# A planned recurrence with attention work in its gaps: a bar on long GpSimd operations, new guesses for DMA, deeper buffers at the start

## The chip, the cores and the metric

The kernel runs on one core of one Trainium2 chip. The metric is the device time of one launch in microseconds (us); lower is better. The engines are TensorE (PE, with its weight loads shown apart as PEld), VectorE (DVE), ScalarE (ACT), GpSimd (POOL) and SyncE (SP, which here issues every DMA). Each engine works through its own list of instructions in the order in which they were written and waits at the head of that list for what it needs.

## The reference, cut to what matters

Eight images of 56x56 positions and 256 channels pass through three layers; `_gn` and `_ln_t` are normalizations over groups and over channels.

```python
x = x + _L0_conv_ref(_gn(x), ...)                  # attention over 4 chosen regions of 8x8
t = _to_tokens(x)                                  # (8, 3136, 256)
t = t + _L1_attn_ref(_ln_t(t), ...)                # each token looks at 7 neighbours
t = t + _L1_ffn_ref(_ln_t(t), ...)                 # a recurrence over the 3136 tokens
# the recurrence, for all 8 images at once
i_t = sigmoid(xi_t + h @ V_i)
g_t = tanh(xg_t + h @ V_c)
o_t = sigmoid(xo_t + h @ V_o)
c_new = h * c + i_t * g_t                          # f_t isn't used
h_new = o_t * tanh(c_new)
```

In the first layer each of 49 regions takes the 4 regions whose mean keys fit best. Each of the 64 queries of a region, in each of 8 heads, keeps the 32 largest of 256 scores, and a softmax over those weighs the values. A depthwise 3x3 convolution of the values is added before the output projection.

## The kernel before, in words

**Units.** The image is cut into 7 rows of 7 regions (448 tokens each). A unit is one such row of one image, and the units run through all 8 images before the next row: 56 units. For a unit the kernel loads the row (`xn`), projects queries and values, writes the values to DRAM and reads them back three times shifted (`lines`, then `vshift`), convolves them with 24 matmuls on PE (`convolve`), and handles 7 regions (`region`: gather keys and values by DMA, scores on PE, eight rounds of MAX8 and MATCH_REPLACE8 per pair of heads on DVE, three Exp on ACT, a subtraction `pe<-pe,left` of 128x256 on POOL, transposes and products on PE). Behind it come the output projection, the attention over 7 neighbours and the input part of the gates, `gates`, which adds a bias on POOL (`gs<-gs,bu`) and writes the result to DRAM (`xgd`). I call all of this row work.

**The start.** For each image `norm_and_route` first reads the image in 7 chunks of 448 KB for statistics (`stats`), then in 7 chunks again (`keys_values`): a chunk `xchunk` is normalized on DVE, four matmuls make its keys (`ks`) and eight its values, ACT copies these out as four tiles `vs` and SP writes each to DRAM (`vd<-vs`). `xchunk`, `ks` and `vs` have two buffers each. The norm of the images is spread over the first units.

**The recurrence.** One step has a chain of six operations: 16 matmul records that add `h @ V` to a PSUM bank (`r_sum`), a DVE transpose (`r_tr`), a tanh on ACT (`r_cell<-r_tr`), a DVE scan (`r_c`), a tanh on ACT (`r_tc`), and a DVE operation that makes the new h (`r_hs`). Beside the chain, POOL makes the next step's product h*c (`r_cell<-r_hs,r_half`), which the next scan reads; I call it POOL's part. The terms `xgd` are loaded eight tokens at a time (`r_gin`) by SP and copied into the PSUM bank by ACT (`place_terms`). From step 2688 on, when only the recurrence is left, the matmuls for o are done apart (`step_apart`). `follow` records the steps of a row when the row's terms have been recorded, so a step at a multiple of 448 needs what the last unit of a row has written.

**The planner.** Nothing is written to the engines directly. `_Plan.record` collects every operation with its reads and writes, a guess `held` of how long it occupies its engine and a guess `late` of when its result is there (`_time`). `_Plan.run` then walks through a model time and hands each free engine the first ready operation by rank: the recurrence has rank 0, its six operations are marked `chain`, row work has rank 1. An operation that isn't of the chain is taken only if its end lies before the time at which the chain is expected to need that engine, plus `SLACK`. For POOL the expected time is that of the next chain operation on DVE with more than one tile read, which are the scan and the `r_hs` operation. Where PE would idle for over 250 ns a small matmul into `spare` is written. `at` counts the chain operations handed out, so `at % 6` is the place within a step: 0 behind `r_hs`, 1 behind the matmuls, 4 behind the scan. What comes out is one fixed order for each engine; on the chip the guesses no longer count, only the order and the real waits.

All recorded operations carry line 290 in the profile, so groups are told apart by their tiles.

Of the kernel before, what the change touches and what calls it, by code (L numbers as in the profile page):

```python
# [10 lines left out]
F32 = mybir.dt.float32  # L11
# [46 lines left out]
HOP = 70  # L58
FAR = 10**12
FILL = 250  # L60
SLACK = {"PE": 120, "DVE": 120, "ACT": 60, "POOL": 60, "SP": 1000}


def _shape_of(shape, pattern, sizes):
# [37 lines left out]
def _time(engine, name, view, reads, args, kw):  # L102

    n = max([_count(v) for v in [view] + reads])
    if engine == "SP":
        return 650, 2600 + n // 2
    if engine == "PE":
        held = 160 if name == "transpose" else 5 * _count(view) // 3 + 110
        return held, held + 200
    if engine == "POOL":  # L110
        t = 180 + 15 * n // 7
        return (1050, 1050) if ALU.pow in args else (t + 90, t)
    if engine == "ACT":
        t = 5 * n // 7 + 100
        if kw.get("accum_out") is not None:
            return t + 150, t + 260
        if isinstance(kw.get("bias"), _View) or view.buf.banks:
            return t + 120, t + 200
        return t + 20, t + 110
    held = 25 * n // 24 + 60  # L120
    if name == "reciprocal":
        return 20 * n // 3 + 60, 20 * n // 3 + 150
    if name == "transpose":
        return held + 40, held + 120
    if name == "tensor_tensor_scan":
        return 2 * n + 80, 2 * n + 170
    if name == "match_replace":
        return held + 65, held + 150
    if name == "scalar_tensor_tensor":
        return held + 20, held + 100  # L130
    return held, held + 90
# [97 lines left out]
class _Plan:  # L229
# [112 lines left out]
    def run(self, tc, fill):  # L342
        ops = self.ops
        for tag in self.tags.values():
            for i, buf in enumerate(tag):
                kin = [b for b in tag[:i] if b.stream == buf.stream][-1:] if buf.free else tag[i - 1 : i]
                before = [(b.users[0], 0) for b in kin]
                if i >= buf.bufs and not buf.free:
                    before += [(u, None) for u in tag[i - buf.bufs].users]
                for u, gap in before:  # L350
                    for v in buf.users:
                        if u is not v:
                            g = gap
                            if g is None:
                                g = u.held if u.engine == v.engine else u.late + HOP
                            u.before[v] = max(g, u.before.get(v, 0))
        for op in ops:
            op.open, op.due = 0, 0
        for op in ops:
            for b in op.before:  # L360
                b.open += 1
        engines = ("PE", "DVE", "ACT", "POOL", "SP")
        free = dict.fromkeys(engines, 0)
        later = {e: [] for e in engines}
        ready = {e: [] for e in engines}
        chain = [o for o in ops if o.chain]
        at, made, events = 0, {}, []

        def opened(op):
            heappush(later[op.engine], (op.due, op.rank, op))  # L370
            heappush(events, op.due)

        for op in ops:
            if not op.open:
                opened(op)
        done, now = [], 0

        def expected(engine):


            t = None
            for k in range(at, min(at + 7, len(chain))):
                op = chain[k]
                if t is None:
                    if op.open:
                        break
                    t = max(op.due, now)
                else:
                    p = chain[k - 1]
                    t += p.late + (HOP if p.engine != op.engine else 30)  # L390
                if op.engine == engine or engine == "POOL" and op.pair:
                    return t
            return FAR

        filled = 0
        while len(done) < len(ops) + filled:
            moved = False
            for e in engines:
                if free[e] > now:
                    continue  # L400
                while later[e] and later[e][0][0] <= now:
                    _, rank, op = heappop(later[e])
                    insort(ready[e], (rank, op))
                if not ready[e]:
                    continue
                until = expected(e) + SLACK[e]
                for i, (rank, op) in enumerate(ready[e]):
                    if not op.chain and now + op.held > until:
                        continue
                    if any(b.free and not self._room(b, made, now) for b in op.takes):  # L410
                        continue
                    del ready[e][i]
                    op.start = now
                    free[e] = now + op.held
                    heappush(events, free[e])
                    heappush(events, now + op.late + HOP)
                    done.append(op)
                    for b in op.takes:
                        if b.free:
                            made.setdefault(id(b.tag), []).append(b)  # L420
                    for b, gap in op.before.items():
                        b.due = max(b.due, now + gap)
                        b.open -= 1
                        if not b.open:
                            opened(b)
                    if op.chain:
                        at += 1
                    moved = True
                    break
            if not moved and free["PE"] <= now:  # L430

                due = min([expected("PE")] + [op[0] for op in later["PE"][:1]])
                if FILL < due - now < FAR // 2:
                    op = _Op()
                    op.trace, op.start = [fill], now
                    filled += 1
                    done.append(op)
                    free["PE"] = now + FILL
                    heappush(events, free["PE"])
                    moved = True  # L440
            if not moved:
                while events and events[0] <= now:
                    heappop(events)
                if not events:
                    raise RuntimeError("the plan has stopped")
                now = heappop(events)
        self.length = now
        with tc.manual_schedule():
            for op in done:
                for t in op.trace:  # L450
                    t()
# [25 lines left out]
def _layers(ctx: ExitStack, tc, a, out):  # L477
# [154 lines left out]
    def norm_and_route(b, im):  # L632
# [1 line left out]


        def chunk(p):
            xc = two.tile([P, 2, ROW], F32, name="xchunk")
            nc.sync.dma_start(
                xc, xt[b, :, p * ROW : (p + 1) * ROW].rearrange("(k q) s -> q k s", k=2)
            )  # L640
            return xc
# [67 lines left out]
        def keys_values(p):  # L709
            xn = chunk(p)  # L710
            normalize(im, xn)
            ks = two.tile([P, NWIN, 2, S], F32, name="ks")
            for m in range(2):
                pk = bank()
                for k in range(2):
                    nc.tensor.matmul(
                        pk[:, :ROW], w0[:, k, C + m * P : C + (m + 1) * P],
                        xn[:, k, :], start=(k == 0), stop=(k == 1),
                    )
                nc.scalar.activation(  # L720
                    ks[:, :, m, :], pk[:, :ROW].rearrange("p (q s) -> p q s", s=S),
                    AF.Identity, bias=b0[:, 2 + m : 3 + m],
                )
            nc.sync.dma_start(
                im["kd"][p * NWIN : (p + 1) * NWIN].rearrange("q p s -> p q s"),
                ks.rearrange("p q k s -> p q (k s)"),
            )
            for i in range(NQB):
                pv = bank()
                for k in range(2):  # L730
                    nc.tensor.matmul(
                        pv[:QB, :C], xn[:, k, i * QB : (i + 1) * QB], w0[:, k, 2 * C :],
                        start=(k == 0), stop=(k == 1),
                    )
                vs = two.tile([QB, C], F32, name="vs")
                nc.scalar.copy(vs, pv[:QB, :C])
                t0 = p * ROW + i * QB
                nc.sync.dma_start(im["vd"][t0 : t0 + QB], vs)
# [773 lines left out]
```

## Time and profile before

| what | value |
|---|---|
| median of 3 runs | 9912.33 us (9910.28 to 9922.73) |
| profiled execution | 9902.77 us, its span 9901.1 us |
| 0 to 1500 us (before the recurrence) | PE busy 1239.49 us, DVE 1052.58 us, granted clock 0.90 |
| 1500 to 8890 us (row work and recurrence) | PE busy 6891.83 us, DVE 6562.68 us, POOL 2691.74 us |
| 8890 us to the end (recurrence alone) | PE busy 872.89 us, DVE 432.97 us |
| steps of the recurrence | 3136 |

The busy times come from the profile's table by stretches of the span. Busy PE includes the `spare` matmuls, which do nothing for the result. A mean duration of a group can hide two populations, so places where it matters are looked at in the timeline, whose columns are start in us, length in us, engine, line, operation, output<-inputs, shape and count, and in brackets how long the engine had been idle and who ended that.

### The profile page before, as it was taken

Reading aid. Unit: us, or ns where it says so; the run is one execution under the profiler, and the core shown is the slowest. Engines: PE = TensorE matmul, PEld = TensorE weight load, DVE = VectorE, ACT = ScalarE, POOL = GpSimd, SP = SyncE. Lnnn points to the kernel's source line nnn. Section 1 sums busy time; section 2 is a strip of 40 time slices with the busy share of each in tenths; the row PEclk is TensorE's granted clock in tenths of the full one; section 3 lists DMA queues with packets and bytes.
Section 4 is the critical chain, followed back from the end, with each engine's and each line's share of the span. In section 5 each row is a group of like instructions: output and inputs, shape, how many; then the busy total and the mean of one; then the engine's idle time right before and its main releaser. Section 6 shows DMA issues by size and latency. Waiting matters only on the chain.

```text
span 9901.1 us, 320002 instructions
## 1 busy us (share of the span) xinstructions
PE 9004.2 (91%) x111782; PEld 5270.8 (53%) x111782; DVE 8048.2 (81%) x32969; ACT 5863.0 (59%) x22855; POOL 3193.8 (32%) x7550
## 2 busy tenths in 40 slices
PE   6888889999999999999999999999999999998888
PEld 4445445555555555555545555555555545557777
DVE  5686688999998999989989899898988888874444
ACT  3444456666666666666666666666666666654444
POOL 1222233333333333333333333333333333331111
PEclk9989889999999999999999999999999999999999
DMA  5544423233233232332323323233232222220000
GB/s 156 150 131 132 121 82 86 75 80 82 76 82 81 71 83 77 81 81 71 84 74 81 81 72 86 74 81 79 74 85 76 72 73 79 75 53 21 21 21 19
DMA packets 838243, 786.81 MB, mean 79 GB/s; under 512 B 94734, under 2 KB 794244, under 8 KB 836628
## 3 DMA queue, kind: packets, MB, share of 16 engines
q1 hardware_dynamic: 836628, 766.33, 29.1%
q8 instruction: 884, 14.48, 0.6%
q14 instruction: 731, 5.99, 0.2%
HBM read 527.08 MB, written 238.88 MB: 77 GB/s over the span
## 4 chain that ended last, share of the span: by engine, by line
DVE 46%; PE 16%; ACT 12%; DMA 5%; issue 5%; SPq 1%; POOL 1%; DVEq 0%; ACTq 0%; POOLq 0%
DVE left L290 13%; DVE top L290 10%; PE r_sum L290 9%; DVE r_c L290 7%; DVE r_tr L290 7%; ACT r_cell L290 5%; PE mm L290 5%; DVE r_hs L290 4%; DMA vshift<-lines 2%; ACT r_tc L290 2%; DMA lines<-v 2%; PE pt_av L290 1%; DVE st L290 1%; PE spare L604 1%; ACT et L290 1%
## 5 line engine op out<-in xcount | busy, mean ns | idle before, releaser
L290 PE MATMUL r_sum<-r_v,r_hs 128*8 128x192 f32 (+1 forms) x57376 | 2650.4, 307 | 496.1 <-DVE r_hs L290 439.1
L290 POOL TENSOR_TENSOR r_cell<-r_hs,r_half 128x16 f32<-128x16 f32 x3136 | 722.6, 230 | 4643.2 <-DVE r_hs L290 2588.8
L604 PE MATMUL spare<-ident 128*32 128x128 f32 x15904 | 2208.1, 277 | 1.5 <-POOL ident masks.py:199 1.5
L290 ACT ACTIVATE r_cell<-r_tr 128x48 f32<-128x48 f32 (+2 forms) x3587 | 911.7, 259 | 2156.4 <-DVE r_tr L290 2069.5
L290 PEld LDWEIGHTS r_sum<-r_v,r_hs 128*8 128x8 f32 x57376 | 1233.5, 89 | 1739.1 <-DVE r_hs L290 1397.5
L290 DVE MATCH_REPLACE8 left<-top,left 128x256 f32<-128x256 f32 x4704 | 1899.5, 407 | 0.2 <-issue 0.2
L604 PEld LDWEIGHTS spare<-ident 128*32 128x32 f32 x15904 | 1596.3, 110 | 471.9 <-issue 373.2
L290 DVE MAX8 top<-left 128x8 f32<-128x256 f32 x4704 | 1841.1, 406 | 1.4
L290 DVE STREAM_TRANSPOSE r_tr<-r_sum 128x192 f32<-128x192 f32 (+2 forms) x3587 | 1231.9, 350 | 631.1 <-PE r_sum L290 607.0
L290 DVE TENSOR_TENSOR_SCAN r_c<-r_cell 128x48 f32<-128x48 f32 x3136 | 945.5, 302 | 542.3 <-ACT r_cell L290 382.3
L290 POOL TENSOR_TENSOR pe<-pe,left 128x256 f32<-128x256 f32 x1568 | 1142.1, 733 | 731.2 <-ACT left L290 590.7
L290 ACT ACTIVATE r_tc<-r_c 128x16 f32<-128x16 f32 x3136 | 701.1, 224 | 508.9 <-DVE r_c L290 469.9
L290 ACT COPY r_sum<-r_gin 128x384 f32<-128x384 f32 (+2 forms) x1795 | 807.7, 450 | 14.1 <-DMA r_gin<-xgd 7.8
L290 ACT ACTIVATE pe<-sc,nmax 128x256 f32<-128x256 f32 x1568 | 684.9, 472 | 173.0 <-DVE left L290 103.4
L290 PE MATMUL pt_av<-ident,pe 128*128 128x128 f32 x3136 | 690.5, 297 | 91.2 <-POOL pe L290 67.2
L290 ACT ACTIVATE left<-left,nmax 128x256 f32<-128x256 f32 x1568 | 749.1, 500 | 35.5 <-DVE left L290 26.3
L290 DVE SCALAR_TENSOR_TENSOR r_hs<-r_cell,r_tc 128x16 f32<-128x16 f32 x3136 | 587.9, 187 | 188.8 <-ACT r_tc L290 183.7
L290 PE MATMUL mm<-wu,xlT 128*112 128x512 f32 (+2 forms) x1856 | 728.1, 509 | 3.2 <-ACT gs L290 2.5
L290 ACT ACTIVATE et<-top,nmax 128x32 f32<-128x32 f32 x1568 | 497.3, 318 | 332.8 <-DVE top L290 325.4
L290 DVE MAX8 top<-sc 128x8 f32<-128x256 f32 x1568 | 618.2, 412 | 78.6 <-PE sc L290 75.2
L290 ACT COPY pts<-pt_av 128x256 f32<-128x256 f32 x1568 | 566.0, 361 | 169.5 <-PE pt_av L290 166.8
L290 ACT ACTIVATE r_half<-r_c 128x16 f32<-128x16 f32 x3136 | 651.4, 208 | 0.0
(128 smaller groups left out, 11793.0 us busy)
## 6 DMA issues: line engine op xcount, KB each, us to landing
kg<-kd SPq DMA_DIRECT2D x1568, 64.0 KB
vg<-vd SPq DMA_DIRECT2D x1568, 64.0 KB
vshift<-lines SPq DMA_DIRECT2D x336, 232.0 KB
xgd<-gs SPq DMA_DIRECT2D x224, 336.0 KB
r_gin<-xgd SPq DMA_DIRECT2D x1568, 48.0 KB
xchunk<-xt SPq DMA_DIRECT2D x112, 448.0 KB
lines<-v SPq DMA_DIRECT2D x112, 290.0 KB
xn<-xh SPq DMA_DIRECT2D x56, 560.0 KB
```

What stands on the lines that cost most here:

```text
L290: method(*[v.real() if isinstance(v, _View) else v for v in args], **{k: v.real() if isinstance(v, _View) else v for k, v in kw.items()},)
L604: raw.tensor.matmul(spare[:32, :P], ident[:, :32], ident, start=True, stop=True, skip_group_check=True)
```

## The change

Four edits, all in the planner and in three buffer counts:

- In `_Plan.run`, an operation of POOL with a guessed length over 400 ns isn't taken while `at % 6 > 3` (behind the scan, before the `r_hs` operation), nor while a counter `tied` is below `at // 6`. `tied` counts POOL's operations of rank 0 outside the chain.
- `SLACK` of PE goes from 120 to 60 ns.
- The guess for a DMA of n elements per partition goes from 2600 + n/2 to 2400 + 9n/4 ns.
- `xchunk` has 4 buffers, `ks` 3 and `vs` 4, in place of 2 each.

```diff
-SLACK = {"PE": 120, "DVE": 120, "ACT": 60, "POOL": 60, "SP": 1000}
+LONG = 400
+SLACK = {"PE": 60, "DVE": 120, "ACT": 60, "POOL": 60, "SP": 1000}
...
     if engine == "SP":
-        return 650, 2600 + n // 2
+        return 650, 2400 + 9 * n // 4
...
-        filled = 0
+        filled = tied = 0
...
                     if not op.chain and now + op.held > until:
                         continue
+                    if e == "POOL" and op.held > LONG and (at % 6 > 3 or tied < at // 6):
+
+                        continue
...
                     if op.chain:
                         at += 1
+                    elif e == "POOL" and op.rank[0] == 0:
+                        tied += 1
...
-            xc = two.tile([P, 2, ROW], F32, name="xchunk")
+            xc = two.tile([P, 2, ROW], F32, name="xchunk", bufs=4)
...
-            ks = two.tile([P, NWIN, 2, S], F32, name="ks")
+            ks = two.tile([P, NWIN, 2, S], F32, name="ks", bufs=3)
...
-                vs = two.tile([QB, C], F32, name="vs")
+                vs = two.tile([QB, C], F32, name="vs", bufs=4)
```

No operation of the computation is added or removed. Of the engines' lists, all but PE's hold the same operations in another order; PE's has 255 `spare` matmuls fewer (7697 for 7952).

## The prediction

> **What bounds the kernel now.** I read the busy times by stretch first, then the waits of the middle stretch, then the timeline where the longest waits stand.
>
> ```profile
> 0.00:1500.00 1500.00, 1239.49 (x8038) 711.87 (x8042) 1052.58 (x3975) 677.82 (x2039) 395.97 (x724) 0.90 0.46 129
> 1500.00:8890.00 7390.00, 6891.83 (x84875) 3817.68 (x84864) 6562.68 (x27133) 4752.23 (x18559) 2691.74 (x6368) 1.00 0.30 77
> 8890.00:9900.00 1010.00, 872.89 (x18896) 741.20 (x18884) 432.97 (x1862) 432.98 (x2259) 106.06 (x458) 1.00 0.09 21
> ```
>
> Behind stretch and length stand busy PE, PEld, DVE, ACT, POOL, the granted clock, the DMA share and GB/s. Before 1500 us PE is the busiest; from then on the recurrence never stops, so its 3136 steps are the path. I took the start and length of all six chain operations of every step from the trace. With the medians of the stretch (r_hs to matmuls 55 ns, matmuls 837, 67 to the transpose as the shortest usual gap, 366, 94, tanh 268, 101, scan 258, 34, tanh 223, 32, r_hs 174) a step takes 2509 ns; the mean is 2752. Over steps 50 to 2685 the excess is some 630 us: 169 in front of the matmuls, 21 in them, 146 in front of the transpose, 135 inside the scan, 41 inside r_hs, the rest in small parts. The last 451 steps take 1005 us and the change touches nothing there.
>
> The 169 us are three things. Six waits of 10 to 12 us (63 us in all) stand where a new row's first terms are needed, every 448 steps:
>
> ```profile
> 2707.08 0.35 SPq L290 DMA_DIRECT2D xgd<-gs  x1
> ...
> 2708.58 0.16 DVE L290 SCALAR_TENSOR_TENSOR r_hs<-r_cell,r_tc 128x16 f32<-128x16 f32 x1
> ...
> 2713.37 2.68 SPq L290 DMA_DIRECT2D r_gin<-xgd  x8
> ...
> 2718.64 0.90 ACT L290 COPY r_sum<-r_gin 128x384 f32<-128x384 f32 x2 [2.08 <-DMA xgd<-gs]
> ...
> 2719.18 0.84 PE L290 MATMUL r_sum<-r_v,r_hs 128*8 128x192 f32 x16 [1.80 <-ACT r_sum L290]
> ```
>
> From the write of the terms to their use pass 12.1 us, and the write stands one step ahead of the use. Next, 51 waits over 0.5 us make 70 us; most look like this:
>
> ```profile
> 3208.36 0.44 DVE L290 SCALAR_TENSOR_TENSOR r_hs<-r_cell,r_tc 128x16 f32<-128x16 f32 x1
> ...
> 3210.61 1.16 PE L290 MATMUL mm<-vshift,diag 96*32 96x448 f32 x8 [3.44 <-DMA vshift<-lines]
> ...
> 3212.62 1.30 PE L290 MATMUL r_sum<-r_v,r_hs 128*8 128x192 f32 x12
> ...
> 3214.32 0.38 DVE L290 STREAM_TRANSPOSE r_tr<-r_sum 128x192 f32<-128x192 f32 x1 [4.13 <-PE r_sum L290]
> ```
>
> The convolution stands in PE's list before its data has landed, the step's matmuls are queued behind it, and then run at half speed (1.9 us for 0.84): that is the 21 us. The waits name it:
>
> ```profile
> DVE r_tr L290 <- PE r_sum L290: 264.9, 345, 6.3
> ...
> PE mm L290 <- DMA vshift<-lines: 78.2, 50, 4.1
> ```
>
> What is left of the 169, waits of 5 to 500 ns, is 36 us. At the start each chunk of keys and values has this cycle:
>
> ```profile
> 79.50 0.65 ACT L290 COPY vs<-mm 112x256 f32<-112x256 f32 x2 [2.16 <-DMA vd<-vs]
> ...
> 79.92 3.27 PE L290 MATMUL mm<-xchunk,w 128*128 128x448 f32 x8 [1.31 <-ACT vs L290]
> ...
> 83.03 3.73 PE L290 MATMUL mm<-w,xchunk 128*112 128x256 f32 x16
> ...
> 88.06 3.27 PE L290 MATMUL mm<-xchunk,w 128*128 128x448 f32 x8 [1.29 <-ACT vs L290]
> ```
>
> 8.14 us per chunk for 7.0 us of PE. The slow scans are those that meet a long POOL operation:
>
> ```profile
> 5003.66 0.73 POOL L290 TENSOR_TENSOR pe<-pe,left 128x256 f32<-128x256 f32 x1 [1.24 <-ACT left L290]
> ...
> 5003.85 0.64 DVE L290 TENSOR_TENSOR_SCAN r_c<-r_cell 128x48 f32<-128x48 f32 x1 [0.15 <-ACT r_cell L290]
> ...
> 5005.11 0.23 POOL L290 TENSOR_TENSOR r_cell<-r_hs,r_half 128x16 f32<-128x16 f32 x1 [0.72 <-DVE r_hs L290]
> ```
>
> The scan is held until 0.10 us behind POOL's end. The long operation stands in POOL's list ahead of the r_cell of the same step, and its inputs are there early, so nothing holds it back until that step's r_hs.
>
> **The bar on long POOL operations.** Matched to the planner's list, 529 of the 535 slow scans (over 290 ns) and all 191 slow r_hs (over 200 ns) meet a long operation that was handed out at place 0 of a step, before that step's POOL part. In the list of before 1225 of 2741 long ones stand so. The bar should forbid them, but its counter also counts the memset of `r_hs` that opens the first block (POOL, rank 0, outside the chain): `tied` runs one ahead, and an operation ahead of POOL's part is still let through. In the changed list 1228 of 2739 stand there. Only the 38 behind the scan are gone, and those make 0.4 us of slow scans. I take 0. Between the ends: all 176 us gone (that is a rival below), or a few us more when POOL runs earlier. Nothing new queues behind a barred operation: r_cell, nmax and the rest pass it.
>
> **PE's slack.** Of the 36 us, what lies above 60 ns in waits of 60 to 500 ns is about 20 us. The row work that caused it has to stand elsewhere. From 0 to -36 I take -12.
>
> **The DMA guesses.** For `vshift` (n = 1856) the guess goes from 3528 to 6576 ns, for `lines` from 2890 to 3705. From issue to landing I find, by the semaphores, a median of 3.9 us for vshift behind the end of its issue, with a tenth over 8.6. In the lists the convolution moves from a median of 9 chain operations behind its last vshift load to 15 (least 7 to 13): at 2752/6 = 459 ns, from 4.1 to 6.9 us. About 85% of the late ones are then in time: 0.85 x (70 + 21) = 77. Ends 0 and -91; I take -77. What is late next is the tenth over 8.6 us. The page DMA: Bandwidth & Descriptors of the Trainium skill (section Anatomy of one DMA) fits another issue path with 2.0 us + bytes/436e3; as an estimate 2.5 us for the 232 KB of a vshift load, which the old guess already covered, so by it the new one would be worth 0 and the sum 77 us smaller; the 3.9 us and the 50 waits speak against it.
> For the row's first terms: the write for the last unit's first block stands at step 445.0 for the first row (444.8 before), but at 888.8, 1336.8, 1784.8 and 2231.2 for the next (892.8, 1340.8, 1788.8, 2236.8), and at the last border the loads stand 3 to 5 steps ahead of their use instead of in the wait. Four steps are 11 us of the 12.1. I leave 12 for the first, 1.5 for each of four, 0 for the last: 18 of 63, so -45 (ends 0 and -63). `x<-x` waits on POOL (43.6 us) shorten too; the scan waited for POOL only 10.5 us in all, so I take 0 (end -11).
>
> **The buffers.** `vs` with four: ACT's 81.2 us in 51 waits for vd go, and PE's 52.5 us behind them, in a stretch that PE sets (a unit with a norm takes 168 us, one without 112; the difference is seven chunk cycles). 51 x about 0.9 = 45 is the part I take, since units overlap other waits; ends 0 and -82. `xchunk` with four: DVE waits 227.6 us for these loads, under a PE that is busier; 0, and if PE stops covering, part of it comes back as time. `ks`: no wait on it in the trace, 0. These loads and writes move up in SP's list past other issues; that price is in a rival.
>
> **Sum.** -12 - 77 - 45 - 45 = -179 against the profiled execution's 9902.8: 9724. The median of the runs lies 9.5 above that execution: **9733 us**, 1.8% less. Its own range, with half of each term lost or the ends reached, is 9650 to 9820.
>
> **Rivals.**
> 1. The convolution's waits stay, because SP issues the loads late rather than their landing being slow: SP works in order, and 8.6 us for the last tenth is no transfer of 232 KB. Without the 77 us: 9810.
> 2. Row work takes the place: DVE is 89% busy in the middle, and if the chain's gain of 77 + 12 + 45 returns as longer waits at the row borders, only the start's 45 remains: 9867. Against it: the lists put the borders' writes four steps earlier.
> 3. The bar works as its words say: 176 us more, 9557. The count of 1228 speaks against it.
> 4. Slower: at the start up to four chunk loads stand in front of the gathers, lines and xn that a unit waits for in turn. A chunk takes a median of 3.4 us to land and up to 14.5; two more ahead of each of some four such waits are 27 us per unit, over 8 units 218 us: 9733 + 218 = 9951. It decides from 22 us per unit (179/8). For it: x1s loads land in 7.4 us there and in 3.1 later. Against: the DMA share there is 0.46.
>
> **How the numbers follow.** Likeliest 0.53, rival 1 0.10, rival 2 0.15, rival 3 0.04, rival 4 0.15, no change 0.03. About 0.2%, 20 us, is what this kernel's runs can tell from no change. Rival 2's upper edge reaches no change: faster 0.80, same 0.05, slower 0.15. The range takes in the likeliest and rivals 1 and 2: with every end reached the sum is -283, so 9630; above, 9890; outside lie rivals 3 and 4.
>
> **What would show it.** Right: PE's wait for vshift from 78 to under 20 us; six border waits with only the first near 10 us; the recurrence starting at about 1455 us instead of 1500; ACT's wait for vd near 0; scans in the middle still at a mean of about 309 ns, against these 257 ns without POOL's work:
>
> ```profile
> L290 DVE TENSOR_TENSOR_SCAN r_c<-r_cell 128x48 f32<-128x48 f32 x444 | 114.2, 257 | 113.0 <-ACT r_cell L290 113.0
> ```
>
> Wrong: a scan mean near 260 (rival 3), a first step after 1500 us (rival 4), border waits over 15 us (rival 2), the vshift wait unchanged (rival 1).

## The result, and the profile after

The changed kernel takes 9620.9 us (median of four runs, 9618.41 to 9625.59) against 9917.5 us before (four runs, 9910.28 to 9936.62). The ratio is 0.9699, with a 95% interval from 0.9682 to 0.9715: 3.0% less, 297 us, where 1.8% was forecast.

The profiled execution has a span of 9619.5 us. The busy times by stretch, columns as before:

```profile
0.00:1500.00 1500.00, 1298.88 (x9363) 766.59 (x9364) 1149.37 (x4331) 750.27 (x2279) 431.42 (x803) 0.92 0.48 134
1500.00:8890.00 7390.00, 6967.58 (x88303) 3886.18 (x88303) 6567.28 (x27296) 4802.47 (x18953) 2688.34 (x6421) 1.00 0.29 77
8890.00:9619.00 729.00, 628.09 (x13614) 534.90 (x13608) 312.31 (x1344) 310.98 (x1624) 73.12 (x326) 1.00 0.08 20
```

In the first 1500 us every engine has done more: PE 1299 us of work for 1239, DVE 1149 for 1053, because the recurrence sets in earlier. The window of the middle now holds all that is left of the row work and the first 280 us of the recurrence alone, and the last stretch ends earlier because all of it starts earlier. Taken from the `r_hs` operations of the two traces:

| stretch | before | after | difference | forecast |
|---|---|---|---|---|
| start to the first step | 1500.2 us | 1407.7 us | -92.5 | -45 |
| first to 2686th step | 7391.1 us | 7202.1 us | -189.0 | -134 |
| the rest | 1005.1 us | 1005.2 us | 0 | 0 |

Both parts gained more than forecast: the start about twice as much, the rows 1.4 times. The waits of the middle stretch (columns: us in total, times, longest), of which these two are what is left of the ones that mattered:

```profile
DVE r_tr L291 <- PE r_sum L291: 230.9, 389, 1.5
...
POOL v L291 <- DMA lines<-v: 32.0, 19, 7.8
```

PE's wait for `vshift`, 78.2 us in 50 waits before, has no line any more, and the longest wait of the transpose for the step's matmuls fell from 6.3 to 1.5 us. The second row border of the timeline, whose step took 13.0 us before:

```profile
3791.18 3.41 SPq L291 DMA_DIRECT2D xgd<-gs  x2
...
3794.68 3.12 SPq L291 DMA_DIRECT2D r_gin<-xgd  x8
...
3803.57 0.18 DVE L291 SCALAR_TENSOR_TENSOR r_hs<-r_cell,r_tc 128x16 f32<-128x16 f32 x1
...
3805.00 0.92 ACT L291 COPY r_sum<-r_gin 128x384 f32<-128x384 f32 x2
...
3805.76 0.84 PE L291 MATMUL r_sum<-r_v,r_hs 128*8 128x192 f32 x16
```

The write stands 13.8 us ahead of the copy, and the chain makes five `r_hs` in that time; in the piece shown of before it was 11.6 us with one `r_hs` in them, and the rest was waiting. This step takes 4.5 us. The first border stayed bad; there the write still stands behind the last step that can run:

```profile
2589.82 0.18 DVE L291 SCALAR_TENSOR_TENSOR r_hs<-r_cell,r_tc 128x16 f32<-128x16 f32 x1
...
2595.71 2.04 SPq L291 DMA_DIRECT2D xgd<-gs  x2
...
2605.06 0.95 ACT L291 COPY r_sum<-r_gin 128x384 f32<-128x384 f32 x2
2606.39 0.83 PE L291 MATMUL r_sum<-r_v,r_hs 128*8 128x192 f32 x16
```

The six border steps take 18.8, 4.5, 4.5, 4.5, 2.9 and 2.2 us, in place of 12.6 to 14.2 each. In the start the chunk cycle is 6.57 us, where it was 8.14:

```profile
71.53 3.17 PE L291 MATMUL mm<-xchunk,w 128*128 128x448 f32 x8
...
74.53 3.73 PE L291 MATMUL mm<-w,xchunk 128*112 128x256 f32 x16
...
78.10 3.17 PE L291 MATMUL mm<-xchunk,w 128*128 128x448 f32 x8
```

No gap is left behind the value matmuls. The waits of the first 1400 us, before:

```profile
POOL v L290 <- DMA lines<-v: 98.5, 6, 78.2
...
PEld mm L290 <- ACT vs L290: 81.8, 77, 4.8
ACT vs L290 <- DMA vd<-vs: 81.2, 51, 4.1
```

and after:

```profile
POOL v L291 <- DMA lines<-v: 18.1, 5, 6.8
...
PEld mm L291 <- ACT vs L291: 13.3, 21, 2.6
...
ACT vs L291 <- DMA vd<-vs: 5.7, 5, 2.1
```

ACT's wait for the value writes falls from 81.2 to 5.7 us and PE's weight loads wait 13.3 us for `vs` instead of 81.8. POOL's wait for `lines`, 98.5 us before, is a change that the prediction didn't look at. Last, the scans (columns: busy us, mean ns, idle before and who ended it), before from 1500 to 8890 us and after from 1500 to 8500 us:

```profile
L290 DVE TENSOR_TENSOR_SCAN r_c<-r_cell 128x48 f32<-128x48 f32 x2684 | 829.1, 309 | 427.6 <-ACT r_cell L290 267.6 <-POOL gs L290 20.8 <-POOL pe L290 5.4
```

```profile
L291 DVE TENSOR_TENSOR_SCAN r_c<-r_cell 128x48 f32<-128x48 f32 x2609 | 786.9, 302 | 412.5 <-ACT r_cell L291 256.3 <-POOL gs L291 16.8 <-ACT r_sum L291 7.2
```

302 ns for 309: 480 scans are still slow, and 478 of them meet a long POOL operation that stands ahead of that step's `r_cell`. The bar has hardly touched them.

### The profile page after: what moved, and what is told of

It is laid out like the page before. It is cut to its first block, busy times and chain, and to the rows that moved or that the text cites. A ratio compares the mean times of both kernels' runs of the same rounds, so it can differ in the third digit from the quotient of the medians.

```text
span 9619.5 us, 318746 instructions
## 1 busy us (share of the span) xinstructions
PE 8894.6 (92%) x111272; PEld 5187.7 (54%) x111272; DVE 8029.0 (83%) x32969; ACT 5863.7 (61%) x22855; POOL 3192.9 (33%) x7550
## 4 chain that ended last, share of the span: by engine, by line
DVE 49%; PE 16%; ACT 12%; issue 5%; DMA 2%; POOL 2%; DVEq 0%; SPq 0%; ACTq 0%; POOLq 0%
DVE left L291 14%; DVE top L291 12%; PE r_sum L291 9%; DVE r_c L291 8%; DVE r_tr L291 7%; ACT r_cell L291 5%; PE mm L291 5%; DVE r_hs L291 4%; ACT r_tc L291 2%; PE spare L610 1%; DVE st L291 1%; ACT et L291 1%; PE pt_av L291 1%; ACT pe L291 1%; DVE t L291 1%
## 5 line engine op out<-in xcount | busy, mean ns | idle before, releaser
L610 PE MATMUL spare<-ident 128*32 128x128 f32 x15394 | 2161.8, 277 | 1.5 <-POOL ident masks.py:199 1.5
L610 PEld LDWEIGHTS spare<-ident 128*32 128x32 f32 x15394 | 1533.2, 110 | 479.5 <-issue 387.3
L291 ACT ACTIVATE pe<-sc,nmax 128x256 f32<-128x256 f32 x1568 | 683.6, 473 | 115.1 <-DVE left L291 78.2
L291 PE MATMUL mm<-wu,xlT 128*112 128x256 f32 (+2 forms) x1856 | 722.9, 509 | 6.0 <-ACT xlT L291 5.7
L291 PEld LDWEIGHTS pt_av<-ident,pe 128*128 128x128 f32 x3136 | 363.7, 144 | 526.9 <-issue 297.1
```

Of the source, the lines that this page charges most:

```text
L291: method(*[v.real() if isinstance(v, _View) else v for v in args], **{k: v.real() if isinstance(v, _View) else v for k, v in kw.items()},)
L610: raw.tensor.matmul(spare[:32, :P], ident[:, :32], ident, start=True, stop=True, skip_group_check=True)
```

## The experiments

Every kernel was run beside the one before on the same chip; the ratio is to that. "First" is the first step, "rows" the time from there to the 2686th, "borders" the sum of the six border steps, "wait" what stands in front of the matmuls above the usual 55 ns, "hold" the excess of scan and `r_hs` over 258 and 174 ns. These come from one profiled execution each; of the kernel without the bar, profiled twice (e_nobar and e_nobar2), they give a first step of 1406 and 1413 us and rows of 7214 and 7210 us, so differences of a few us say nothing.

| kernel | us | ratio [95%] | first | rows | borders | wait | hold |
|---|---|---|---|---|---|---|---|
| before | 9917.5 | | 1500 | 7391 | 78 | 186 | 179 |
| changed | 9620.9 | 0.9699 [0.9682, 0.9715] | 1408 | 7202 | 38 | 46 | 169 |
| e_buf | 9845.7 | 0.9947 [0.9932, 0.9963] | 1433 | 7394 | 81 | 179 | 182 |
| e_vs | 9852.8 | 0.9930 [0.9914, 0.9947] | 1463 | 7412 | 81 | 200 | 182 |
| e_xchunk | 9919.4 | 0.9997 [0.9988, 1.0007] | 1509 | 7408 | 78 | 198 | 180 |
| e_guess | 9738.9 | 0.9834 [0.9819, 0.9849] | 1452 | 7275 | 38 | 62 | 174 |
| e_slack | 9782.1 | 0.9881 [0.9866, 0.9896] | 1503 | 7268 | 45 | 80 | 164 |
| e_noslack | 9650.5 | 0.9727 [0.9711, 0.9743] | 1413 | 7236 | 18 | 44 | 174 |
| e_nobar | 9631.5 | 0.9726 [0.9712, 0.9739] | 1406 | 7214 | 49 | 54 | 177 |
| e_count | 9716.8 | 0.9799 [0.9782, 0.9816] | 1414 | 7302 | 271 | 322 | -3 |
| e_pool | 9708.3 | 0.9787 [0.9771, 0.9803] | 1401 | 7296 | 93 | 104 | 174 |
| e_count3 | 9546.3 | 0.9629 [0.9612, 0.9646] | 1403 | 7135 | 92 | 120 | 4 |

The changed kernel once more, on one chip with e_count and e_count3 (e_after), took 9618.3 us, ratio 0.9700 [0.9686, 0.9714], and the one without the bar there (e_nobar2) 9630.7 us, 0.9713 [0.9699, 0.9728].

### The buffers: e_buf, e_vs, e_xchunk

The kernel before, with all three buffer counts (e_buf), with one line alone (e_vs), with another alone (e_xchunk):

```diff
+            xc = two.tile([P, 2, ROW], F32, name="xchunk", bufs=4)
+            ks = two.tile([P, NWIN, 2, S], F32, name="ks", bufs=3)
+                vs = two.tile([QB, C], F32, name="vs", bufs=4)
```

> The kernel before with the three buffer counts alone. In its lists the part behind the start of the recurrence is unchanged. Theory A (the start's 93 us, 1500 to 1408, come from the buffers alone): first step at about 1410 us, rows as before (7391 us from the first to the 2685th step), in all about 9825 us. Theory B (the buffers give the 45 us that the prediction took, the rest comes from the new DMA guesses in the start's order): first step at about 1455 us, in all about 9870 us.

> The kernel before with four buffers for vs alone. The three counts together brought the first step from 1500 to 1433 us. If ACT's wait for vd is what the start lost (81 us there, 52 us of PE behind it): first step at about 1450 us, in all about 9915 - 50 = 9865 us. If the chunk loads matter more: first step near 1485 us, 9900 us.

> The kernel before with four buffers for xchunk alone. The prediction's value is 0: first step at 1500 us, 9915 us. If DVE's 228 us of waits for these loads were on the path in part: first step at about 1480 us, 9895 us; the two single counts then add up to the 67 us of all three.

All three together are worth 56 us by the medians; `vs` alone is worth 66 (the intervals overlap), `xchunk` alone nothing (between -12 and +7 us). So the gain is that of `vs`, as forecast, and it comes in the start: the first step of e_buf stands 67 us earlier, its rows take as long as before. (The profiled execution of e_buf is the fastest of its four runs, 7 us under their median.) That of e_vs is the slowest of its four, 34 us over their median, so its first step shows less. In e_buf the waits of the first 1400 us are

```profile
DVE xchunk L290 <- DMA xchunk<-xt: 108.3, 17, 13.8
...
ACT vs L290 <- DMA vd<-vs: 7.4, 5, 2.2
```

DVE's wait for `xchunk` is 57 us shorter than before (164.8), and e_xchunk, where four buffers for it gain nothing, speaks for the reading that PE covers that wait.

### The DMA guesses: e_guess

```diff
-        return 650, 2600 + n // 2
+        return 650, 2400 + 9 * n // 4
```

> The kernel before with the new DMA guesses alone. If the waits of the convolution and at the row borders come from the guesses: waits in front of the step's matmuls fall from 181 us to about 50, PE's wait for vshift from 78 us to under 20, first step at 1500 us or a little later, in all about 9915 - 140 = 9775 us. If SP's lateness and not the guess makes the convolution wait: vshift wait stays near 78 us, in all about 9860 us.

This one line is worth 163 us, more than half of the change. It alters the guess of every DMA at once, so the shares of the single transfers aren't separated. In its lists the convolution stands a median of 15 chain operations behind the last `vshift` load, as in the changed kernel, and PE's wait for `vshift` has no line. Five borders take 2.9 to 5.6 us, the last 20.4. That is the mechanism that was forecast, at -116 us in the rows. What was not forecast is the start: the first step stands 48 us earlier with two buffers everywhere. The wait of POOL for `lines` in the first 1400 us, 98.5 us before (78.2 of it one wait), is here

```profile
POOL v L290 <- DMA lines<-v: 10.0, 3, 5.2
```

and 97.0 us in e_slack, whose start is no shorter; but in e_buf it is 104.5 us and the start is 67 us shorter, so this wait alone doesn't set the start. By the last `xgd` write of each unit, the second unit of e_guess takes 141 us instead of 165, the third to seventh 0 to 9 us less each, the eighth 4 us more. The trace doesn't give one wait that all of this could be put down to, and no run here separates it.

### PE's slack: e_slack on the kernel before, e_noslack on the changed one

```diff
-SLACK = {"PE": 120, ...}
+SLACK = {"PE": 60, ...}
```

e_noslack has this undone in the changed kernel.

> The kernel before with PE's slack of 60 ns alone. Prediction's term: 12 us for the slack itself; the border writes also stand four steps earlier in this list (887.8 for 892.8), which would give up to 40 us more; the vshift wait stays near 70 us. About 9915 - 12 - 40 = 9863 us. If slack costs row work its place: border waits above 10 us, 9915 us or more.

> The changed kernel with PE's slack back at 120 ns. New guesses alone took 116 us from the middle, the smaller slack alone 124, both in the changed kernel 189. If both cure the same waits (convolution and row borders), leaving the slack out costs only the difference: 189 - 116 = 73 us, in all about 9694 us, vshift waits near 0 and border waits below 45 us in sum. If the slack acts on its own: 9621 + 120 = 9741 us.

Alone the slack is worth 120 us, ten times the forecast; on top of the rest it is worth some 30 (27 by the ratios, whose intervals just overlap). The account of the steps says where. In e_slack the short waits that the forecast was about (60 to 500 ns in front of the matmuls) fall from 34 to 21 us, about the -12 that was forecast. But the long ones fall as well, borders from 78 to 45 us and PE's wait for `vshift` from 78.2 to

```profile
PE mm L290 <- DMA vshift<-lines: 26.5, 24, 3.0
```

because the list came out differently: the convolution stands 12 chain operations behind its last load (median; 10 before, 15 with the new guesses), and the row's first terms are written at step 887.8 instead of 892.8. With the guesses in place there is nothing left of that to gain: e_noslack has borders of 18 us and 0.4 us of PE waiting for `vshift`. Against the changed kernel it has 16 us more of short waits and 29 us more in front of the transposes, and 20 us less at the borders. Why a smaller slack on PE moves the write of the terms by five steps was not separated; the planner hands out every engine's work by one model clock, so one number reaches all lists, but that is argued, not shown.

### The bar: e_nobar, e_count, e_pool, e_count3

e_nobar and e_nobar2 are the changed kernel without the bar:

```diff
-                    if e == "POOL" and op.held > LONG and (at % 6 > 3 or tied < at // 6):
-
-                        continue
```

> The changed kernel without the bar on long operations of POOL. If the bar does nothing because its counter runs one ahead: 9621 us within 15 us, scan mean in the middle about 300 ns in both. If the 45 long operations behind the scan that come back cost what fell between the two profiles inside the scan and ahead of r_hs (135 to 115 and 62 to 42 us): about 9621 + 40 = 9661 us.

> The changed kernel without the bar, once more and on the same chip as the changed kernel. If the bar is worth nothing, the two agree within 10 us; if the 12 us between the two profiles' middle stretches (7202 and 7214 us) are real, this one is slower by 10 to 15 us.

> The changed kernel once more, so that it can be set beside the next three on one chip: 9621 us within 15 us.

The bar as it is saves 11 and 12 us, some 0.12%, in the two comparisons (9631.5 against 9620.9, and 9630.7 against 9618.3 on one chip, with no overlap of the runs). Most of it isn't what its words say: 11 us are the border sum (the last border 2.2 us for 11.8). The hold, which its words are about, is 8 us smaller in the first pair of profiles and 1.5 us in the second (171.6 against 173.1). e_count mends its counter, so that the memset of `r_hs`, the only kind of POOL operation of rank 0 outside the chain that opens a buffer, is no longer counted:

```diff
-                    elif e == "POOL" and op.rank[0] == 0:
+                    elif e == "POOL" and op.rank[0] == 0 and not op.takes:
```

> The changed kernel with the bar's counter mended, so that it leaves out the memset: in the list no long operation of POOL stands between r_hs and that step's r_cell any more (0 for 1228). Theory A (the slow scans and slow r_hs come from these, and nothing else depends on their place): scan mean 258 ns, r_hs 174, in all 9621 - 169 = 9452 us. Theory B (POOL needs the place: there are 1.02 long operations per step, and behind r_cell the planner fits only one in front of the scan): the scans do get fast, but row work is late and the waits at the row borders grow from a sum of 38 us to over 200; in all 9620 to 9720 us.

Now the bar does what it says. In the list no long operation stands ahead of its step's `r_cell` (1228 did), and the scans of 1500 to 8500 us of e_count are

```profile
L291 DVE TENSOR_TENSOR_SCAN r_c<-r_cell 128x48 f32<-128x48 f32 x2593 | 672.1, 259 | 389.3 <-ACT r_cell L291 259.4 <-POOL r_cell L291 9.1 <-ACT r_sum L291 2.0
```

259 ns, 9 slow ones, hold -3 us where it was 179 before: the 176 us of the third rival are there, whole. And the kernel is 98 us slower than the changed one, since 234 us came back at the borders. The second border of e_count:

```profile
3792.65 0.17 DVE L291 SCALAR_TENSOR_TENSOR r_hs<-r_cell,r_tc 128x16 f32<-128x16 f32 x1
...
3800.28 0.73 POOL L291 TENSOR_TENSOR v<-v,bv 118x256 f32<-118x256 f32 x1 [3.30 <-ACT v L291]
...
3811.01 2.00 PE L291 MATMUL mm<-wu,xlT 128*112 128x512 f32 x2
...
3819.86 2.59 SPq L291 DMA_DIRECT2D xgd<-gs  x2
...
3831.77 0.88 ACT L291 COPY r_sum<-r_gin 128x384 f32<-128x384 f32 x2
```

When the recurrence runs out of terms, the last unit still has part of its second attention, its normalization and its gates to do; 27 us pass before the terms are even written. Row work has fallen behind. The list tells where: there are 2739 long POOL operations for 2685 steps, 1.02 per step, and 2399 of them stand at one place, directly behind the handing out of the step's matmuls (173 one place earlier, 167 one later). If a step has room for one of them, POOL can just not keep up; the next run tests that. e_count3 keeps the mended counter and makes room for a second one in a step, by a shorter guess for POOL's operations and more slack; e_pool has the shorter guess alone, in the changed kernel with its counter as it is:

```diff
-SLACK = {..., "POOL": 60, ...}
+SLACK = {..., "POOL": 200, ...}
...
-        return (1050, 1050) if ALU.pow in args else (t + 90, t)
+        return (1050, 1050) if ALU.pow in args else (t, t)
```

> The mended counter, and the planner's view of POOL widened so that two long operations fit behind r_cell: the guessed length of a POOL operation 90 ns shorter (818 to 728, measured 733) and POOL's slack 200 ns for 60. Theory B: the border waits shrink to under 80 us in sum while the scans stay near 258 to 270 ns; about 9560 us, faster than the changed kernel. Theory A would give the same as for the run before, 9452 us. If two in a row reach into the scan after all: scan mean 300 ns and no gain, 9620 us or more.

> The changed kernel with the guessed length of POOL's operations 90 ns shorter, the counter as it is. A control for the run with the mended counter and a wider view of POOL (9546 us). If the gain there is from the place of the long operations, here some 1146 of them stand ahead of r_cell again, the scan mean is about 300 ns and the time 9600 us or more. If it is from the guess: about 9550 us.

e_count3 takes 9546.3 us, 3.7% less than before and 72 us less than the changed kernel beside it: the fastest of all. Its scans are

```profile
L291 DVE TENSOR_TENSOR_SCAN r_c<-r_cell 128x48 f32<-128x48 f32 x2646 | 692.6, 262 | 420.7 <-ACT r_cell L291 237.7 <-POOL gs L291 16.0 <-POOL pe L291 12.7
```

649 long operations now stand at the later place, three borders are down to 2.7 to 2.8 us, one takes 15 and two take 33 to 35 us. The hold is 4 us for 169, and the borders give back 54. e_pool is 87 us slower than the changed kernel, so the shorter guess by itself does harm; the gain of e_count3 goes with the place of the long operations, once they fit. The slack of POOL was not tried apart, so what it adds by itself is not shown.

## Why the prediction was right or wrong

**What failed.** The time is 112 us under the forecast (9621 for 9733) and 29 us under the lower end of the range. By the two profiles the start gave 48 us more than its term and the rows 55 more than theirs. Two steps of the sum failed: the start was priced with the waits for `vs` alone, at 45 us, and the DMA guesses were put at nothing there; and 36 us of the rows were in no term. What the waits for `vs` left out is shown below; why the guesses shorten the start, and where the 36 us come from, stay open.

**The direction and the main mechanism were right.** The convolution's waits went: PE's wait for `vshift` from 78.2 us to no line, longer waits in front of the matmuls away from the borders from 86 to about 2 us, the excess of the matmuls from 21.8 to 8.5 us. Together that is -97 against -77. (86 is what is over 500 ns, 149 us, less the 63 us of the borders; after, 24 less 22.) Two readings made the term too small. The 169 us end one step before the last border, while the 63 us hold its 12 us; so the rest of 70 us for the convolution came out 12 too small (52 such waits in those steps make 82 us), and the first 50 steps hold another 4. And the 15% that I left late, for loads over 8.6 us, are not late because there is no such tenth: by the 16 semaphore increments of each load, the 282 loads of the middle land a median of 3.7 us behind the end of their issue, a tenth over 5.0, and one over 8.6. PE's waits end 0.135 us behind the landings read this way. The estimate from the fit in the Trainium skill (DMA: Bandwidth & Descriptors, section Anatomy of one DMA), by which the old guess was enough and the new one worth 0, doesn't hold for these loads, and the fit is for another issue path: the median is 3.7 us for the estimated 2.5, and PE's wait for `vshift` went with the new guesses alone. One number of that paragraph was wrong: the convolution of the kernel before stands a median of 10 chain operations behind its load, not 9 (9 is the quarter point).

**The borders were right.** -45 was forecast, 78.4 to 37.5 us is -41. Which ones would stay was right too, but the first grew to 18.8 us where I left 12.

**The short waits of PE's slack were right, the term wasn't.** They fell by 14 us for -12. But the step "From 0 to -36 I take -12" bounded the edit by the waits that it names, and it reaches the borders and the convolution through the lists: -120 alone, -30 on top of the rest. For the sum this did less harm than it looks, because the guesses cure the same waits.

**The start was the largest miss of a term**: -93 for -45. `vs` with four was priced at 51 x 0.9 us = 45, because units overlap other waits; the cycle became 6.57 us, and e_buf shows -67 by itself, within the ends of 0 and -82. The traces show what the term left out. Up to the first `r_hs` PE has the same work before and in e_buf (7178 matmul records outside `spare`, whose ends the profile models). In e_buf PE is idle 34 us less (199 for 233), and that same work keeps it busy 28 us less (1074 for 1102). Most of this is in the key matmuls `mm<-xchunk,w`, which stand behind the waits for `vs` (202 to 178 us, each counted from the end of the one before). So the term counted the waits and not that the matmuls behind them ran longer; why they did isn't separated. The guesses were given no term in the start at all, and have -48 there alone, 30 of it idle time of PE and 19 shorter work. The two overlap by about 22 us (67 + 48 - 93). That a DMA guess also orders the first 1500 us is the step that was missing.

**The remaining 36 us of the middle were in no term**: scans -19, the wait between the second tanh and `r_hs` -20, the wait in front of the transposes -10, in front of the first tanh -7, against +8 in front of the scan and +10 in `r_hs`, with 2 us in the rest. No run separates these; e_nobar has the first three nearly as well (-11, -16, -15), so most of them isn't the bar's.

**The sum.** In the two profiled executions the difference is -282 where -179 was forecast, and by the medians the gain is 297. The prediction's sum with every end reached was -283, at 9630, but its range stopped at 9650. That -283 and -282 meet is luck: the start and the convolution went beyond their ends (-93 for -82, -97 for -91) and 36 us were in no term, while the borders and the slack stayed short of theirs. The parts alone give -56, -163, -120 and -12, in sum -351: they overlap by 54 us.

**The rivals.** The first, loads issued too late, is out: no wait for `vshift` is left. The second, row work as the bound, is out for this kernel: the borders shrank, although DVE is now busy 6531 of the 7202 us of the rows, 91% for 89%. In e_count row work does come late at the borders, though. The third was rightly held unlikely, for the right reason: 1228 long operations let through, hold 169 us for 179. But its price of 176 us looked at the scans alone and named nothing that would be late next; the mended bar costs 98 us against the changed kernel, and only e_count3 nets part of that price (72 us). The fourth, a slower start behind the deeper buffers' loads, is out: the first step came at 1408 us, and e_xchunk is within 0.1% of before.

## What to carry to other kernels

In a kernel whose instruction order is planned with guessed latencies, one guess that is too short shows up as many waits at the head of an in-order list, far from the transfer itself; look for operations that stand in a list before their data can be there, and price the guess on every stretch that it orders, the start included, and with a wait price the matmuls behind it. An edit to such a planner can't be bounded by the waits that it is meant for: PE's slack alone took 13 us out of its own and some 107 out of the rest. And when work is barred from a place, count first how many places per step are left and how many are needed: 1.02 long operations per step didn't fit into one place, and the waits that went came back where the row's result was due.

## What the runs showed of the hardware

The hold of a scan is very regular: of the 480 slow scans in the changed kernel, half end between 0.113 and 0.115 us behind the end of the POOL operation that they meet, 9 in 10 between 0.111 and 0.116 us. As in this piece of the timeline, with 5002.59 + 0.73 against 5003.01 + 0.42:

```profile
5002.59 0.73 POOL L291 TENSOR_TENSOR pe<-pe,left 128x256 f32<-128x256 f32 x1
5003.01 0.42 DVE L291 TENSOR_TENSOR_SCAN r_c<-r_cell 128x48 f32<-128x48 f32 x1 [0.46 <-ACT r_cell L291]
```

The Trainium skill (SBUF — State Buffer, section "A bandwidth-pool intuition that's wrong (but worth ruling out)") describes such a wait in the other direction, GpSimd's writing of DMA descriptors held until some 115 ns behind the end of a VectorE operation; the 0.113 us here, with VectorE as the one that waits, agree with it in size. The delay isn't the same for every operation that waits: the 197 slow `r_hs` operations of the same execution (over 200 ns) end a median of 0.032 us behind the POOL operation that they meet, 9 in 10 between 0.029 and 0.034 us. No run here shows what the two engines share.
